# A GNN-and-experts kernel: per-group sums kept as three bf16 parts, and expert tiles taken up in four lots

## The chip, the cores and the metric

The kernel runs on one core of a Trainium2 chip, as one program with one launch. The metric is the device time of that core in microseconds (us).

## The reference

There are N = 6250 rows of D = 512 floats, E = 100000 edges sorted by their target, and 8 experts.

```python
def sage(h, Ws, Wn, b):                      # two layers of this
    agg = segment_sum(h[src], dst, N)        # sum over each row's incoming edges
    deg = segment_sum(1, dst, N)
    return relu(h @ Ws + (agg / max(deg, 1)) @ Wn + b)

x = x + sage(sage(layernorm(x), ...1), ...2)
t = layernorm(x)
top2 = top_k(t @ Wg, 2); gate = softmax(top2 values)
y_e = layernorm(relu(t @ W1[e] + b1[e]) @ W2[e] + b2[e]) * gamma[e] + beta[e]
x = x + sum over the two chosen e of gate_e * y_e
```

All is in float32. The kernel brings in the experts only for the rows that chose them: 12500 row copies, sorted by expert into 105 tiles of 128 rows.

## The kernel before, in words

**Stages.** (0) The layer norm of `x` is written to `xn_d`. (1) The first sums: `sums(xn_d, ...)` with `layer1` as what follows each block. (2) The second sums: `sums(z2, ...)` with `route`, and with work on expert tiles mixed in by `each`. (3) The final loop over the expert tiles that are left, and the gathering of results.

**Sums (L200 to L311).** The 782 tiles of 128 edges are worked in 197 slots, four tiles a slot. Per tile GpSimd issues one indirect DMA (`gather`, L220) that brings 128 rows of 512 floats; VectorE makes a slot's 0/1 matrices `hot` (L230); TensorE adds the four tiles into four strips of 32 rows of the accumulator `pa` (`add`, L248). Three slots make a group, and `close` copies `pa` to SBUF (`st_`, L256): a strip of sums of up to 128 neighbouring rows. A block of 128 rows of the graph needs the three or four groups that `reach` names, 153 pairs of block and group in each sums. `prepare` makes for each pair the 0/1 matrix `sel` (L273, and for the first sums a bf16 copy, L277); `take_out` multiplies it with the strip (L285), so that the block's sums stand in one PSUM tile. The 49 blocks close three to twelve slots, at distances of 3, 3 and 6.

The order on TensorE, VectorE, ScalarE and GpSimd is the program's own (`manual_schedule`). A slot `i` issues the gathers for a later slot (two on in the second sums, where the ring has 12 buffers; three on in the first, with 16), what `each` gives, `build(i + 2)`, `add(i)`, then what is due at place "mid", then `close`, then what is due at "post". `at(i + k, place, what)` puts something k slots on. SP's queue has no order by hand.

**What follows a block.** In the first sums `layer1`: `u0` the own share for blocks below NS = 36, `u1` transposes, `u2` times Wn1, `u3` transposes, `u4` times Wn2 to `z2` through a tile `z` with one buffer (L576), `u5` times Ws2 to `s2` through a tile `s` with one buffer (L583); the last four `u5` come after the loop. Each of these products is four float32 matmuls, which the trace shows as eight instructions. In the second sums `route`: the sum is finished on VectorE (L987, L988), normalized (L182 to L187, L995), turned, and multiplied with Wg; the two experts are chosen (`experts`), ranked, and the row is sent to each expert's list in `xs` by two indirect DMAs (L975). In the first 48 slots `each` also gives the product of the 36 own shares with Ws2 (`share_of`, L907).

**Expert tiles.** `take_up` on VectorE turns the counts so far into a list of tiles that are full already. It runs when the blocks in `TAKE` are through: blocks 16, 27 and 38, which free 24, 46 and 68 tiles in all. From then on `each` starts one tile at every even slot (`Up`): `fetch` from `xs`, `turn_x` 3 slots on, `times` (W1, L818) 5 on, `turn_h` 6 on. Tiles in `soon` (odd numbers, 34) are finished in the sums as well (`Down`): the product with W2 (L852) and the row b2 by a bf16 matmul (L846) 8 slots on, statistics (L858) 9 on, scaling and the rows gamma and beta (L846, in the two PSUM buffers `ph`) with the products y\*g and +b on VectorE (L876, L877) 10 on. The others store their hidden rows in `hd` and get their `Down` in the final loop.

**The final loop** takes the 71 tiles left: 34 whose hidden rows are read back from `hd` (one `Down` each), then 37 that get both `Up` and `Down`. Meanwhile GpSimd makes the last list (`list_rest`, `places`), and from a given tile on the results are gathered (L1075) and added (L1085).

Of the kernel before, what the change touches and what calls it, by code (L numbers as in the profile page):

```python
# [29 lines left out]
F32 = mybir.dt.float32  # L30
# [37 lines left out]
def gnn_moe(ctx, tc, x, src, dst, Ws1, Wn1, gb1, Ws2, Wn2, gb2, Wg, W1, b1, W2, b2, gamma, beta, out):  # L68
# [131 lines left out]
    def sums(z, pool, pap, room, pn, finish, ring, nring, each=None):  # L200

        nslot = (NG - 1) * TS + min(TS, NT_E - (NG - 1) * NQ * TS)
        ahead = nring // NQ - 1
        tiles = [[t for t in range(i // TS * NQ * TS + i % TS, min(NT_E, (i // TS + 1) * NQ * TS), TS)]
                 for i in range(nslot)]
        gathered, hots, few, strips, counts, sels, sels_h, due = {}, {}, {}, {}, {}, {}, {}, {}  # L210
        pa = [None]

        def at(i, place, what):
            due.setdefault((i, place), []).append(what)

        def gather(i):
            if i < nslot:
                for t in tiles[i]:
                    gathered[t] = ring()
                    nc.gpsimd.indirect_dma_start(  # L220
                        out=gathered[t], out_offset=None, in_=z[:, :],
                        in_offset=bass.IndirectOffsetOnAxis(ap=srcT[:, t : t + 1], axis=0))

        def build(i):
            if i >= nslot:
                return
            g, j = divmod(i, TS)
            m = len(tiles[i])
            hots[i] = pool.tile([P, NQ, SW], F32, name="hot", bufs=4)
            nc.vector.tensor_tensor(  # L230
                hots[i][:, :m],
                rel.rearrange("p (c j) -> p j c", j=TS)[:, j, g * NQ : g * NQ + m]
                .rearrange("p (t o) -> p t o", o=1).to_broadcast([P, m, SW]),
                iota_row[:, :SW].rearrange("p (o m) -> p o m", o=1).to_broadcast([P, m, SW]), OP.is_equal)
            if pn is not None and j:

                end = j == TS - 1 or i == nslot - 1
                few[g] = pool.tile([P, NQ, SW], BF16 if end else F32, name=f"few{int(end)}", bufs=1)
                before = hots[i - 1] if j == 1 else few[g, 1]
                nc.vector.tensor_add(few[g][:, :m], before[:, :m], hots[i][:, :m])  # L240
                few[g, j] = few[g]

        def add(i):
            g, j = divmod(i, TS)
            if pa[0] is None:
                pa[0] = pap.tile([P, D], F32, name="pa", bufs=2)
            for q, t in enumerate(tiles[i]):
                nc.tensor.matmul(pa[0][q * SW : (q + 1) * SW], hots[i][:, q], gathered.pop(t), start=(j == 0),  # L248
                                 stop=(j == TS - 1 or t == NT_E - 1), tile_position=(0, q * SW))

        def close(i):

            g = i // TS
            k = len(tiles[i]) * SW
            st = pool.tile([P, D], F32, name="st_", bufs=most)
            nc.scalar.copy(st[:k], pa[0][:k])  # L256
            strips[g] = st, k
            pa[0] = None
            if pn is not None:
                nc.tensor.matmul(pn[:k, 0], few[g].rearrange("p q m -> p (q m)")[:, :k], halves,  # L260
                                 start=True, stop=True)
                counts[g] = pool.tile([P, NDEG], BF16, name="counts", bufs=most + 1)
                nc.vector.tensor_copy(counts[g][:k], pn[:k, 0])
            for b in range(NB):
                if reach[b][1] == g:
                    at(i + 1, "mid", lambda b=b: prepare(b))
                    at(i + 1, "post", lambda b=b: take_out(i + 1, b))

        def prepare(b):
            for g in range(reach[b][0], reach[b][1] + 1):  # L270
                k = strips[g][1]
                sels[b, g] = pool.tile([P, P], F32, name="sel", bufs=most)
                nc.vector.tensor_scalar(sels[b, g][:k], iota_row[:k], float(b * P), node[:k, g : g + 1],  # L273
                                        op0=OP.add, op1=OP.is_equal)
                if pn is not None:
                    sels_h[b, g] = pool.tile([P, P], BF16, name="sel_h", bufs=most)
                    nc.vector.tensor_copy(sels_h[b, g][:k], sels[b, g][:k])  # L277

        def take_out(i, b):
            a, z = reach[b]  # L280
            ps = room()
            for g in range(a, z + 1):
                st, k = strips[g]
                sel = sels.pop((b, g))
                nc.tensor.matmul(ps, sel[:k], st[:k], start=(g == a), stop=(g == z))  # L285
                if pn is not None:
                    nc.tensor.matmul(pn[:, 1], sels_h.pop((b, g))[:k], counts[g][:k], start=(g == a), stop=(g == z))
# [36 lines left out]
    NT = (2 * N + NE * (P - 1)) // P  # L324
    NT0 = (2 * N + P - 1) // P
    SLOTS = NE * R + (NT - NT0) * P
    TAKE = [NB // 3, 27 * NB // 49, 38 * NB // 49]
    upto_n = [(2 * b * P - NE * (P - 1)) // P for b in TAKE]
    n0 = [0] + upto_n

# [1 line left out]
    NTAKE = len(TAKE) + len(LEVEL) + 1  # L332

    NCL = [(2 * b * P + NE * (P - 1)) // P for b in LEVEL]
    soon = [j for j in range(upto_n[-1]) if j % 2]
    xs = dram.tile([SLOTS, D], F32, name="xs")
    hd = dram.tile([upto_n[-1], P, D], F32, name="hd")
    ys = dram.tile([NT * P, D], F32, name="ys")
# [199 lines left out]
    with tc.tile_pool(name="s1", bufs=2, side="right") as pool, \  # L538
# [6 lines left out]
        def layer1(b, pa, pd):  # L545
# [27 lines left out]
            def u4():  # L573
                pz = psp.tile([P, D], F32, name="pm")
                project(pz, own["hT"], wn2, True, True)
                t = pool.tile([P, D], F32, name="z", bufs=1)  # L576
                nc.scalar.copy(t, pz)
                nc.sync.dma_start(z2[r], t[:n])

            def u5():  # L580
                ps = psp.tile([P, D], F32, name="pm")
                project(ps, own["hT"], ws2, True, True)
                t = pool.tile([P, D], F32, name="s", bufs=1)  # L583
                nc.vector.tensor_add(t, ps, bb2)
                nc.sync.dma_start(s2[r], t[:n])

# [211 lines left out]
    class Up:  # L798
# [9 lines left out]
            tc.add_to_no_dep_group("xs", inst.ins)  # L808

        def turn_x(self):  # L810
            self.xT = transposed(self.pool, self.psp, self.xg, AF.Copy,
                                 out=self.pool.tile([P, C, P], F32, name="xgT", bufs=1))

        def times(self):
            _, self.e = read(eof, self.i, [ENG.PE, ENG.DVE], NE - 1)
# [66 lines left out]
    with tc.tile_pool(name="s2", bufs=2, side="right") as pool, \  # L882
# [45 lines left out]
        def route(b, pa):  # L928
# [10 lines left out]
            def logits():  # L939
                pl = psp.tile([NE, P], F32, name="small", bufs=1)  # L940
                for c in range(C):
                    nc.tensor.matmul(pl[:, :n], wg[:, c, :], t["xT"][:, c, :n], start=(c == 0), stop=(c == C - 1))
                t["lT"] = pool.tile([NE, P], F32, name="lT", bufs=1)
                nc.scalar.copy(t["lT"][:, :n], pl[:, :n])

            def experts():
# [41 lines left out]
            nc.vector.scalar_tensor_tensor(acc[:n], a[:n], 0.0, acc[:n], op0=OP.max, op1=OP.add)  # L988
            nc.sync.dma_start(accs[r], acc[:n])
            for e in range(NE):  # L990
                if b == (1 + 3 * e if e < NE // 2 else NB // 4 - 3 + e):
                    load_w2(e)
            mv, rs = norm_stats(pool, acc[:n], n)
            t["xn"] = part(NW + (13, 14, 16)[b % 3])
# [8 lines left out]
        def each(i):  # L1003
# [11 lines left out]
                return []  # L1015
            up_next[0] += 1
            u = Up(j, pool, psp, keep=j not in soon)
            u.fetch()
            todo = [(3, "mid", u.turn_x), (5, "mid", u.times), (6, "mid", u.turn_h)]
            if j in soon:  # L1020
                d = {}

                def begin():
                    d[0] = Down(j, u.hT, u.e, pool, psp, pool.tile([P, D], F32, name="y", bufs=1))
                    d[0].rows = {"gamma": "ph", "beta": "ph"}
                    d[0].times()
# [325 lines left out]
```

## Time and profile before

| | us |
|---|---|
| three runs | 2961.6, 2962.2, 2971.19; median 2962.2 |
| profiled execution, time | 2965.84 |
| profiled execution, span of the profile | 2964.1 |
| TensorE matmul busy | 2710.7 (91%) |
| GpSimd busy | 1846.4 (62%) |
| VectorE busy | 1203.8 (41%) |
| ScalarE busy | 616.8 (21%) |
| first gather of the first sums, first of the second, last of the second | 116.9, 1139.0, 2311.5 |
| first product of the final loop | 2431.6 |

An engine's busy time is the union of its instructions. TensorE's instructions are pipelined and each is shown until its modelled end, so an instruction that is started alone looks longer than one of a dense row. The starts of neighbouring instructions tell what each costs. A name such as `big<-z,srcT` is the written tile and the read ones; `big` is one large SBUF tile that is used in parts of 512 floats (`part`). DMA issues are not counted as an engine's busy time, but GpSimd's indirect ones are shown, since it makes their descriptors.

### The profile page before, as it was taken

The page shows a single profiled execution, that of the slowest core. Times are in us where ns is not written, and L with a number is a line of the kernel's source. Part 1 is how long each engine was busy: PE and PEld are TensorE (multiplying, and loading weights), DVE is VectorE, ACT ScalarE, POOL GpSimd, SP SyncE. Part 2 cuts the span into 40 slices and gives each one's busy share as a digit, 9 for nine tenths or more (in the row PEclk, how much of TensorE's full clock was granted, in tenths as well). Part 3 has the DMA queues.
Part 4 walks back from the last instruction along what each step waited for, and adds up shares of the span by engine and source line. Part 5 has one row for each costly group of instructions (what it writes and reads, how often), then busy time and mean ns, then how long its engine had stood idle before and what let it go on. Part 6 is the DMA issues. An engine that isn't in the chain of part 4 may idle for free. (4 is left out here: it accounts for less than half of the span.)

```text
span 2964.1 us, 33569 instructions
## 1 busy us (share of the span) xinstructions
PE 2710.7 (91%) x9704; PEld 1063.8 (36%) x9704; DVE 1203.8 (41%) x4163; ACT 616.8 (21%) x1127; POOL 1846.4 (62%) x2116
## 2 busy tenths in 40 slices
PE   6899999999999997999878999999899889999994
PEld 3333333333333332333212333333333333344441
DVE  6522222222222221343334445444544436544775
ACT  2211111111111110111112333333233312222221
POOL 5377777777777763777777777677677128200543
PEclk9999999999999998999999999999999989999997
DMA  6778888888877765999888888888788324312986
GB/s 229 246 241 249 250 247 250 275 251 249 245 238 234 238 208 180 324 325 324 270 283 275 283 276 270 263 264 264 242 271 267 123 86 149 115 60 69 303 292 209
DMA packets 269818, 699.12 MB, mean 236 GB/s; under 512 B 43036, under 2 KB 43150, under 8 KB 269596
## 3 DMA queue, kind: packets, MB, share of 16 engines
q0 software_dynamic: 144000, 464.43, 51.0%
q1 hardware_dynamic: 121964, 225.61, 22.0%
q10 hardware_dynamic: 3664, 6.85, 0.7%
q8 instruction: 83, 1.36, 0.2%
q14 instruction: 107, 0.88, 0.1%
HBM read 557.23 MB, written 140.28 MB: 235 GB/s over the span
## 5 line engine op out<-in xcount | busy, mean ns | idle before, releaser
L220 POOL DMA_INDIRECT big<-z,srcT x782 | 752.4, 962 | 340.3 <-issue 145.3
L220 POOL DMA_INDIRECT rows_t<-xn_d,srcT x782 | 743.3, 950 | 286.6 <-issue 112.8
L852 PE MATMUL py<-w,hT 128*128 x840 | 392.6, 611 | 16.8 <-DMA hT<-hd 8.6
L248 PE MATMUL pa<-big,hot 128*32 128x512 f32 x1564 | 321.9, 621 | 60.1 <-DMA big<-z,srcT 45.0
L552 PE MATMUL pm<-wn,tT 128*128 128x512 f32 x752 | 347.7, 605 | 0.6 <-ACT tT L196 0.6
L818 PE MATMUL ph<-big,xgT 128*128 x544 | 268.1, 638 | 38.8 <-DVE y L876 38.4
L248 PE MATMUL pa<-rows_t,hot 128*32 128x512 f32 x1564 | 271.0, 609 | 29.5 <-DMA rows_t<-xn_d,srcT 27.3
L1075 POOL DMA_INDIRECT big<-ys,yrow x98 | 107.7, 1099 | 293.9 <-DMA ys<-y 197.0
L852 PEld LDWEIGHTS py<-w,hT 128*128 128x128 f32 x840 | 152.8, 192 | 217.5 <-issue 172.9
L552 PEld LDWEIGHTS pm<-wn,tT 128*128 128x128 f32 x752 | 135.2, 189 | 213.2 <-issue 173.1
L818 PEld LDWEIGHTS ph<-big,xgT 128*128 128x128 f32 x544 | 103.9, 201 | 199.3 <-issue 135.1
L829 DVE TENSOR_SCALAR hT<-pt,b1T 128x128 f32<-128x128 f32 x272 | 76.7, 344 | 165.1 <-PE pt L826 161.8
L552 PE MATMUL pm<-ws,big 128*128 128x512 f32 x320 | 143.5, 592 | 0.0
L975 POOL DMA_INDIRECT xs<-big,slot x98 | 99.1, 1012 | 71.1 <-DVE slot L971 50.9
L907 PE MATMUL ph<-w 128*128 128x512 f32 x288 | 135.1, 613 | 4.2 <-DMA w<-in_L_gnn_W_self 4.2
L1115 PE MATMUL ph<-big,xgT 128*128 x296 | 136.9, 605 | 0.0
L248 PEld LDWEIGHTS pa<-big,hot 128*32 128x32 f32 x1564 | 49.3, 109 | 224.7 <-DMA big<-z,srcT 146.7
L566 DVE SCALAR_TENSOR_TENSOR h<-pm,rcnt,big 128x512 f32<-128x512 f32 x49 | 36.8, 750 | 220.5 <-PE pn L260 209.7
L557 DVE TENSOR_TENSOR big<-pm,bb 128x512 f32<-128x512 f32 x36 | 24.9, 692 | 246.7 <-PE pm L552 246.7
L987 DVE SCALAR_TENSOR_TENSOR big<-ph,rcnt,big 128x512 f32<-128x512 f32 (+1 forms) x49 | 36.8, 751 | 216.6 <-PE ph L285 216.6
L230 DVE TENSOR_TENSOR hot<-rel,iota_row 128x128 f32<-128x128 bf16 (+1 forms) x394 | 107.8, 283 | 31.6 <-PE pa L248 14.2
L858 DVE BATCH_NORM_STATS2 st<-py 128x6 f32<-128x512 f32 x105 | 73.0, 695 | 107.6 <-PE py L846 107.6
(653 smaller groups left out, 3321.7 us busy)
## 6 DMA issues: line engine op xcount, KB each, us to landing
xg<-xs SPq DMA_DIRECT2D x105, 256.0 KB
ys<-y SPq DMA_DIRECT2D x105, 256.0 KB
rows_t<-xn_d,srcT POOLq DMA_INDIRECT x782
big<-z,srcT POOLq DMA_INDIRECT x782
z<-z SPq DMA_DIRECT2D x48, 256.0 KB
xa<-in_x SPq DMA_DIRECT2D x48, 256.0 KB
big<-s SPq DMA_DIRECT2D x48, 256.0 KB
accs<-xa SPq DMA_DIRECT2D x48, 256.0 KB
```

Of the source, the lines that this page charges most:

```text
L220: nc.gpsimd.indirect_dma_start(out=gathered[t], out_offset=None, in_=z[:, :], in_offset=bass.IndirectOffsetOnAxis(ap=srcT[:, t : t + 1], a ...
L230: nc.vector.tensor_tensor(hots[i][:, :m], rel.rearrange("p (c j) -> p j c", j=TS)[:, j, g * NQ : g * NQ + m] .rearrange("p (t o) -> p t o" ...
L248: nc.tensor.matmul(pa[0][q * SW : (q + 1) * SW], hots[i][:, q], gathered.pop(t), start=(j == 0), stop=(j == TS - 1 or t == NT_E - 1), tile ...
L552: nc.tensor.matmul(ph, tT[:, c], w[:, c], start=(start and c == 0), stop=(stop and c == C - 1))
L818: nc.tensor.matmul(ph, self.xT[:, c], w1[:, bass.ds(self.e * KD + c * D, D)], start=(c == 0), stop=(c == C - 1))
L829: nc.vector.tensor_scalar(hT[:, c], pt[:, c], b1T[:, bass.ds(self.e * HC + c, 1)], 0.0, op0=OP.add, op1=OP.max)
L852: nc.tensor.matmul(self.py, self.hT[:, c], w2[:, bass.ds(self.e * KD + c * D, D)], start=(c == 0), stop=False)
L858: nc.vector.bn_stats(st, self.py)
L907: nc.tensor.matmul(ps, hT[:, c], ws2[:, c], start=(c == 0), stop=(c == C - 1))
L975: inst = nc.gpsimd.indirect_dma_start(out=xs[:, :], out_offset=bass.IndirectOffsetOnAxis(ap=slot[:n, b, k : k + 1], axis=0), in_=t["xn"][: ...
L1075: nc.gpsimd.indirect_dma_start(out=yk[:n], out_offset=None, in_=ys[: ready[0] * P, :], in_offset=bass.IndirectOffsetOnAxis(ap=yrow[:n, b, ...
L1115: nc.tensor.matmul(ph, u.xT[:, c], w1[:, bass.ds(u.e * KD + c * D, D)], start=(c == 0), stop=(c == C - 1))
```

## The change

1. **Take-outs in bf16 thirds.** `close` rounds the strip to bf16 (`st[0]`). One slot on, at "mid", `rest` subtracts that from `pa` in PSUM, rounds what is left (`st[1]`), and subtracts again (`st[2]`). `take_out` does three bf16 matmuls for each pair in place of one float32 matmul. `sel` is made in bf16 at once, and the copy L277 goes. `take_out` moves from "post" one slot on to "mid" two slots on.
2. **z and s rows in free parts of `big`**, instead of tiles with one buffer each; the transposed tile `xgT` takes the place of `xg`; `lT` goes into a part; `hot` has 3 buffers in the second sums instead of 4.
3. **Four lots of tiles:** at blocks 12, 20, 29 and 38, which free 16, 32, 50 and 68 tiles.
4. **Two of three tiles** of these 68 are finished in the second sums: 45 instead of 34.
5. **Order:** `fetch` comes at the end of its slot; `times`, `turn_h` and the product with W2 one slot earlier; scaling and the rows gamma and beta earlier too. The last four loads of W2 come one block earlier.

```diff
@@ build
-            hots[i] = pool.tile([P, NQ, SW], F32, name="hot", bufs=4)
+            hots[i] = pool.tile([P, NQ, SW], F32, name="hot", bufs=3 if pn is None else 4)
@@ close, prepare, take_out
-            st = pool.tile([P, D], F32, name="st_", bufs=most)
-            nc.scalar.copy(st[:k], pa[0][:k])
+            st = [pool.tile([P, D], BF16, name=f"st_{h}", bufs=most) for h in range(3)]
             strips[g] = st, k
+            nc.scalar.copy(st[0][:k], pa[0][:k])
+            at(i + 1, "mid", lambda pa=pa[0]: rest(st, k, pa))
...
-                    at(i + 1, "post", lambda b=b: take_out(i + 1, b))
+                    at(i + 2, "mid", lambda b=b: take_out(i + 2, b))
+
+        def rest(st, k, pa):
+            nc.vector.tensor_sub(pa[:k], pa[:k], st[0][:k])
+            nc.scalar.copy(st[1][:k], pa[:k])
+            nc.vector.tensor_sub(st[2][:k], pa[:k], st[1][:k])
...
-                sels[b, g] = pool.tile([P, P], F32, name="sel", bufs=most)
+                sels[b, g] = pool.tile([P, P], BF16, name="sel", bufs=most)
...
-                if pn is not None:
-                    sels_h[b, g] = pool.tile([P, P], BF16, name="sel_h", bufs=most)
-                    nc.vector.tensor_copy(sels_h[b, g][:k], sels[b, g][:k])
...
-                nc.tensor.matmul(ps, sel[:k], st[:k], start=(g == a), stop=(g == z))
+                for h in range(3):
+                    nc.tensor.matmul(ps, sel[:k], st[h][:k], start=(g == a and h == 0), stop=(g == z and h == 2))
@@ tables
-    TAKE = [NB // 3, 27 * NB // 49, 38 * NB // 49]
+    TAKE = [12 * NB // 49, 20 * NB // 49, 29 * NB // 49, 38 * NB // 49]
-    soon = [j for j in range(upto_n[-1]) if j % 2]
+    soon = [j for j in range(upto_n[-1]) if j % 3]
@@ layer1
-                t = pool.tile([P, D], F32, name="z", bufs=1)
+                t = part(b if b < NB - LATE else b - LATE)
...
-                t = pool.tile([P, D], F32, name="s", bufs=1)
+                t = part(b - 1 if b < NB - LATE else b)
@@ Up.turn_x
-                                 out=self.pool.tile([P, C, P], F32, name="xgT", bufs=1))
+                                 out=self.xg.rearrange("p (c n) -> p c n", c=C))
@@ route
-                t["lT"] = pool.tile([NE, P], F32, name="lT", bufs=1)
+                t["lT"] = part(NW + 15)[:NE, :P]
...
-                if b == (1 + 3 * e if e < NE // 2 else NB // 4 - 3 + e):
+                if b == (1 + 3 * e if e < NE // 2 else NB // 4 - 4 + e):
@@ each
-            u.fetch()
-            todo = [(3, "mid", u.turn_x), (5, "mid", u.times), (6, "mid", u.turn_h)]
+            todo = [(0, "post", u.fetch), (3, "mid", u.turn_x), (4, "mid", u.times), (5, "mid", u.turn_h)]
...
-                todo += [(8, "mid", begin), (9, "mid", lambda: d[0].spread()), (10, "mid", lambda: d[0].scale()),
-                         (10, "post", lambda: (d[0].affine(), d[0].finish()))]
+                todo += [(7, "mid", begin), (8, "mid", lambda: d[0].spread()), (8, "post", lambda: d[0].scale()),
+                         (9, "post", lambda: (d[0].affine(), d[0].finish()))]
```

More of the change, by code (lines that the diff above doesn't have):

```diff
@@ L209, in sums @@
                  for i in range(nslot)]
-        gathered, hots, few, strips, counts, sels, sels_h, due = {}, {}, {}, {}, {}, {}, {}, {}
+        gathered, hots, few, strips, counts, sels, due = {}, {}, {}, {}, {}, {}, {}
         pa = [None]
@@ L284, in take_out @@
                 sel = sels.pop((b, g))
-                nc.tensor.matmul(ps, sel[:k], st[:k], start=(g == a), stop=(g == z))
+                for h in range(3):
+                    nc.tensor.matmul(ps, sel[:k], st[h][:k], start=(g == a and h == 0), stop=(g == z and h == 2))
                 if pn is not None:
-                    nc.tensor.matmul(pn[:, 1], sels_h.pop((b, g))[:k], counts[g][:k], start=(g == a), stop=(g == z))
+                    nc.tensor.matmul(pn[:, 1], sel[:k], counts[g][:k], start=(g == a), stop=(g == z))
             for behind, place, what in finish(b, ps) if pn is None else finish(b, ps, pn[:, 1]):
```

## The prediction

> **What bounds the kernel now.** I read the page first, then the groups by line, the windows, the chain of waits by engine, and single slots in order of time. The page:
>
> ```profile
> PE 2710.7 (91%) x9704; PEld 1063.8 (36%) x9704; DVE 1203.8 (41%) x4163; ACT 616.8 (21%) x1127; POOL 1846.4 (62%) x2116
> PE   6899999999999997999878999999899889999994
> L220 POOL DMA_INDIRECT big<-z,srcT x782 | 752.4, 962 | 340.3 <-issue 145.3
> L220 POOL DMA_INDIRECT rows_t<-xn_d,srcT x782 | 743.3, 950 | 286.6 <-issue 112.8
> ```
>
> TensorE looks like the bound everywhere. In the first sums it is not. There GpSimd's gathers take 743.3 us and have 286.6 us before them, 47.1 of it one wait ahead of the first (chain of waits). So 982.8 us hold 782 gathers: 1.257 us each, 0.95 of work and 0.30 of issue. The first starts at 116.9 and the last at 1098.8: no gap. GpSimd sets the pace, 5.03 us a slot, and TensorE merely fits in.
>
> The second sums have two halves. Windows (PE, PEld, DVE, ACT, POOL, clock, DMA), and three pieces in order of time:
>
> ```profile
> 1450.00:1500.00 50.00, 40.04 (x116) 10.25 (x116) 17.59 (x84) 8.29 (x15) 38.44 (x44) 0.97 0.78 243
> 2050.00:2100.00 50.00, 46.34 (x198) 19.78 (x197) 22.04 (x83) 14.51 (x28) 36.25 (x42) 1.00 0.85 273
> 2430.00:2570.00 140.00, 138.16 (x339) 51.78 (x339) 85.39 (x210) 32.18 (x60) 95.73 (x184) 0.97 0.44 140
> ```
> ```profile
> 1496.03 1.05 PE L248 MATMUL pa<-big,hot 128*32 128x512 f32 x2 [0.39 <-DMA big<-z,srcT]
> 1497.37 1.04 PE L248 MATMUL pa<-big,hot 128*32 128x512 f32 x2 [0.29 <-DMA big<-z,srcT]
> ...
> 2054.50 1.07 PE L248 MATMUL pa<-big,hot 128*32 128x512 f32 x8
> ...
> 2062.06 0.37 PE L846 MATMUL ph<-gamma,its 24*128 24x512 bf16 x1
> 2062.28 0.37 PE L846 MATMUL ph<-beta,its 24*128 24x512 bf16 x1
> ...
> 2065.90 3.70 PE L818 MATMUL ph<-big,xgT 128*128 x8 [2.25 <-DVE y L876]
> ...
> 2077.01 1.13 PE L285 MATMUL ph<-st__13706,sel 128*128 128x512 f32 x2 [1.41 <-DVE sel L273]
> 2077.97 1.02 PE L285 MATMUL ph<-st__13870,sel 128*128 128x512 f32 x2
> 2078.83 1.02 PE L285 MATMUL ph<-st__14044,sel 128*128 128x512 f32 x2
> ```
>
> Around 1496 a slot's add comes in pairs that wait for their gathers: each pair is "busy" for 1.04 us, though at 2054 all four pairs take 1.07. The 80% of the first window are therefore mostly idle: with 0.99 for an add, 0.87 a strip and 1.35 a block's routing, slots 48 to 73 hold about 2.1 us of real TensorE work in 5.5. GpSimd sets the pace there too: 48 gathers of 1.254 and three pairs of row sends (2.6 us each beyond a gather) make 68 us for 12 slots, 5.67 a slot. From slot 74 (about 1565 us) on the expert tiles run and TensorE decides: from slot 84 to 192 12 slots take 75 us. In the final loop it is dense: 4.38 us a tile from `hd`, 8.96 a tile with both halves.
>
> **The change part by part.** *Take-outs.* A strip costs 0.87 us (2077.97 to 2078.83). gamma to beta is 0.22 between starts, also bf16 with 512 columns; three make 0.65. Alone such a matmul is shown for 0.37, so 1.11 is the other end. I take 0.65: the three stand in a dense row with the same weights. That is 0.22 saved on each of 153 pairs in either sums. In the first sums it is worth nothing while GpSimd paces: 0.
>
> The Trainium skill ("TensorE: Matmul & The Clock Gate", Back-to-back issue gap) gives about 131 ns for a sustained stream with 512 columns, against the 0.22 us between gamma and beta here; by it three would take 0.39 and the second sums would save 0.26 more on each pair, 40 us. The starts here decide.
>
> *The split.* Each of the 131 groups gets two subtractions (0.69 each, by L877, which reads PSUM too) and one ScalarE copy (0.59, L256). In the first sums 152 casts (0.256) go. Both engines have room; what counts is order. DVE waits between the two subtractions for ScalarE, where the copy stands behind `u4`'s or `turn`'s. Queued behind on DVE: `sel`, scaling, hT, later `hot`. The take-out gets a slot for it. In the first sums, behind `u2`'s row (0.75): subtraction, copy, subtraction, `sel` are ready 3.2 us after `u2`, TensorE needs them after 1.55 (add, `u3`): 1.6 us late, three times in 12 slots. TensorE's work there is 4.31 us a slot with the new strips (4.48 now), so 51.7 + 4.9 + about 2 of other waits = 58.6, against GpSimd's 60.3. It fits, narrowly.
>
> More DVE work can slow the making of descriptors: a gather takes 950 ns in the first sums and 962 in the second, where DVE is about twice as busy. 12 ns times 782 is 9 us at most; 0 to 9, I take 2 within the margin below.
>
> The Trainium skill ("SBUF — State Buffer", SBUF: two separate sides) says that GpSimd can't write descriptors while DVE runs a two-port mode, which speaks against more DVE work beside gathers. If every one of the 66 x 1.38 us of subtractions in the first sums shut it out, that would be 91 us as an estimate; the 12 ns above say that little of this is seen.
>
> *z and s in parts.* The end of the first sums:
>
> ```profile
> 1146.19 0.69 DVE L584 TENSOR_TENSOR s<-pm,bb 128x512 f32<-128x512 f32 x1 [3.79 <-DMA s<-s]
> 1157.50 2.79 PE L248 MATMUL pa<-big,hot 128*32 128x512 f32 x12 [13.10 <-DVE hot L230]
> 1159.65 0.95 POOL L220 DMA_INDIRECT big<-z,srcT  x1 [5.97 <-PE pa L248]
> ```
>
> The last s store leaves its one buffer late, lands about 1156.6 among the gathers, and every engine's first step in the next stage waits for it. TensorE is done at 1144.4, four gathers land about 1146. With s outside, the 13th gather does not wait: 5.97 - 0.30 = 5.7 us; the rest is under GpSimd's pace. Bounds 0 to 6, I take 6. The tail's extra slot costs 2 us of split and saves 2 of waiting for `sel`: 0. `xgT`, `lT` and the third `hot` buffer wait for steps a slot back: 0, up to 2 us. The last W2 load now lies 2 slots ahead of the first product with W2: up to 10 us once; with the descriptors I put 4 for both.
>
> *Tiles earlier and more of them.* By the lists, the first tile starts at slot 60, not 74, the last at 200, not 208, and the loop ends after slot 209, not 218. Slots 60 to 196 now: 137 adds 136, 106 strips 92, routing 46, 59 `Up` of 4.52 (3.54 + 0.43 + 0.55) 267, 29 `Down` of 4.38 127; sum 668. They take 845 (1486 to 2331): 51 is the light part before slot 74, 126 are waits, 1.02 a slot. After: 136 + 69 + 46 + 64 x 4.52 + 41 x 4.38 = 720. Waits: the slots become even (4.5 to 6.9 us instead of 2.1 to 8.7), and `sel` is ready a slot ahead (1.4 to 1.9 less a take-out). But gamma and beta take both `ph` buffers, and the next `times` waits until DVE has done y\*g. In 12 slots this falls twice behind `experts` (1.7 us, now 2.25) and twice behind a take-out, whose row needs 3.6 us on DVE first (3.0 each): 9.4 for the 6.2 that I count now. Even slots give some back. Bounds 0.7 and 1.5 a slot, I take 1.1: 151, and 6 for the light slots to 70, where GpSimd paces: 877, 32 more than now.
>
> *What is left behind the last gather.* Now 98 us (2331 to the first fetch at 2428.9), 67 of it work. After: 4 `Down`, 4 `times` and small things, 41, with waits by slots (31 x 13/22) 59: 39 less.
>
> *Final loop.* 11 tiles fewer from `hd`, dense, 4.38 each: 48 less. The list for its later tiles is ready 34 us after its start (GpSimd, 2429 to 2463) and is first read 83 us after it (19 x 4.38), so it stays hidden.
>
> **Sum:** -6 + 4 + 32 - 39 - 48 = -57; 2965.8 becomes 2909, and against the median (3.6 below the profiled time) about 2905.
>
> **The rivals.** *GpSimd keeps the pace* (20%): if the even slots lose little, slots 60 to 196 need only 137 x 5.67 = 777, 100 less: 2805, with half of it 2855. For: 12 slots hold 66.5 of work against GpSimd's 68. Against: `ph` waits can't be hidden in one ordered queue.
>
> *The moved tiles cost what they save* (20%): 1.35 a slot, +34: 2939; with strips at 1.11 each, which would mean that bf16 thirds do not shorten the take-out at all, 49 more on 106 strips, 2954.
>
> *Slower: the split comes last at the take-out* (10%). DVE and ScalarE hand over three times; if every take-out waits W us longer than above, the first sums absorb 0.5 a block and pay (W - 0.5) x 49, the second pay W x 34. It decides from W = 1.0 (24 + 34 = 58); at 2 it is 141 - 57 = +84: 3046. For: 28.2 us of waiting for y between 1600 and 2330 show that DVE's order already stalls TensorE. Against: ScalarE is 21% busy.
>
> **How the numbers follow.** The forecast itself has 50%. Its own range is 1.1 +- 0.4 a slot, 2850 to 2960; half of the first rival lies inside, and what is left out below is the rest of it, above the slower one: I give 2845 to 2955. About 0.3%, 9 us, is what a measurement can tell from no change. Faster than 2953: the forecast, the first rival and most of the second, 0.86; within: 0.05; slower: 0.09.
>
> **What would show it.** Right: gathers of the first sums still 1.254 apart; the 13th gather of the second without the 6 us; strips 0.65 apart; the first `Up` near 1490; slot 197 near 2358; the final loop 48 shorter. Wrong: pauses between gathers of the first sums; take-outs that wait for the second subtraction; `ph` waits above 13 us per 12 slots; a final loop that waits for its list.

## The result and the profile after

The changed kernel takes 3125.3 us (median of four runs, 3120.4 to 3128.6) against 2966.2 for the kernel before (2961.6 to 2971.2): 1.0532 times, interval 1.0513 to 1.0551. Predicted were 2905 us, in a range from 2845 to 2955. It is 159 us slower. The profiled execution took 3120.35 us, its span 3118.2.

The page of the changed kernel, with the rows that answer to those shown of before, the granted clock and the two groups of tile products:

```profile
PE 2704.3 (87%) x10010; PEld 1061.7 (34%) x10010; DVE 1342.6 (43%) x4313; ACT 681.4 (22%) x1257; POOL 1853.2 (59%) x2129
PE   6899999999999989998788788778878887999994
...
PEclk8999999999999999999899988988889888999997
...
L220 POOL DMA_INDIRECT big<-z,srcT x782 | 750.6, 960 | 552.3 <-PE pa L248 306.0
L220 POOL DMA_INDIRECT rows_t<-xn_d,srcT x782 | 743.6, 951 | 284.4 <-issue 118.6
L858 PE MATMUL py<-w,hT 128*128 x840 | 429.4, 658 | 74.4 <-ACT y L876 54.1
L824 PE MATMUL ph<-big,xg 128*128 x544 | 299.6, 702 | 87.9 <-DVE y L882 72.9
```

The last two groups before:

```profile
L852 PE MATMUL py<-w,hT 128*128 x840 | 392.6, 611 | 16.8 <-DMA hT<-hd 8.6
L818 PE MATMUL ph<-big,xgT 128*128 x544 | 268.1, 638 | 38.8 <-DVE y L876 38.4
```

TensorE is busy for the same time as before (2704 against 2711 us) in a span that is 154 us longer. What grew is the idle time in slices 19 to 33, the second sums. There the gathers now wait for TensorE (552 us idle ahead of them, 340 before), and the clock row has more eights. The first sums' gathers are what they were.

The stages, by the starts of TensorE's instructions in the two traces:

| stage | before, us | after, us | change | predicted |
|---|---|---|---|---|
| up to the first add of the second sums | 1157.5 | 1145.7 | -11.8 | -6 |
| slots 0 to 60 | 328.5 | 335.5 | +7.0 | part of +4 |
| slot 60 to the last add | 843.5 | 1064.1 | **+220.6** | +32 |
| last add to the first product of the final loop | 102.1 | 86.2 | -15.9 | -39 |
| final loop's products | 491.4 | 444.5 | -47 | -48 |
| rest | 41.1 | 42.2 | +1 | 0 |

One stage holds the whole miss. The windows of just that stage (us, then busy time and count of PE, PEld, DVE, ACT and POOL, the granted clock, DMA share, GB/s), before:

```profile
1486.00:2329.50 843.50, 761.52 (x3072) 306.44 (x3072) 404.00 (x1633) 239.80 (x422) 596.08 (x684) 0.96 0.82 265
```

and after:

```profile
1481.20:2545.30 1064.10, 861.68 (x3387) 345.51 (x3387) 499.32 (x1864) 280.95 (x497) 594.12 (x680) 0.90 0.68 210
```

Idle time of TensorE rose from 82.0 to 202.4 us (+120.4), busy time by 100.2, and the mean clock fell from 0.96 to 0.90. My sum had 52 us more work (720 against 668). So about 120 of the 221 us are pauses, about 50 are the work that I counted, and about 50 are work that took longer than before. The list of TensorE's waits in that stage says which pauses they are (us in total, times, longest). Before:

```profile
PE ph L818 <- DVE y L876: 28.2, 11, 5.0
...
PE ph L285 <- DVE sel L273: 11.5, 8, 1.6
```

After:

```profile
PE ph L824 <- DVE y L882: 65.4, 34, 2.2
PE py L858 <- ACT y L876: 45.4, 19, 3.8
...
PE ph L290 <- DVE sel L280: 9.0, 8, 3.4
```

The take-outs do not wait longer than before (9.0 us against 11.5): it is not the split at the take-out. The wait for `y` in front of W1 has grown, from 11 times to 34, and a second one has come that the kernel before did not have: the product with W2 waits for ScalarE to have read the one `py` buffer. The two make 82.6 of the 120 us. Waits for ScalarE's copy of a transposed tile add 27.5 (29.4 us in 24 waits, before 1.9); the rest is spread over small ones. TensorE in order of time (start, us, engine, line, operation, tiles, and in brackets the wait ahead of it):

```profile
2228.11 0.37 PE L852 MATMUL ph<-beta,its 24*128 24x512 bf16 x1
2228.42 1.06 PE L248 MATMUL pa<-big,hot 128*32 128x512 f32 x8
2231.16 5.34 PE L824 MATMUL ph<-big,xg 128*128 x8 [1.68 <-DVE y L882]
...
2245.97 6.47 PE L824 MATMUL ph<-big,xg 128*128 x8 [2.16 <-DVE y L882]
2252.36 1.06 PE L248 MATMUL pa<-big,hot 128*32 128x512 f32 x8
2253.36 3.70 PE L858 MATMUL py<-w,hT 128*128 x8
```

The rows gamma and beta take both `ph` buffers, one add follows, and then the next product with W1 needs one of them back. It waits for about 2 us, and then takes 5.34 or 6.47 us in place of the 3.70 that the same eight instructions take at 2253. The windows of the last two products show why (the clock is the third figure from the end):

```profile
2245.97:2252.36 6.39, 6.39 (x8) 2.50 (x8) 1.23 (x4) 0.00 (x0) 3.53 (x4) 0.56 0.92 312
2253.36:2257.00 3.64, 3.64 (x13) 1.45 (x9) 0.00 (x0) 0.24 (x1) 2.71 (x3) 1.00 0.64 160
```

The first ran at a granted clock of 0.56, the second at 1.00. The pause costs its own 2.16 us and 2.8 more behind it. In this stage 24 of 63 products with W1 and 14 of 41 with W2 took over 4.5 us (before: 5 of 59 and 0 of 28), and what they took beyond 3.70 sums to 77.5 us (before 10.6). That is 67 us more, above the 50 by which busy time outgrew the counted work, because the adds, fewer of which now stand alone in pairs, are shown shorter (156 us, before 188). TensorE was at half clock for 211.6 us of it, before for 61.4.

The wait for `py`, with VectorE's queue beside it:

```profile
2267.32 1.06 PE L248 MATMUL pa<-big,hot 128*32 128x512 f32 x8
2267.43 0.75 DVE L993 SCALAR_TENSOR_TENSOR big<-ph,rcnt,big 128x512 f32<-128x512 f32 x1 [4.16 <-PE ph L290]
2268.21 0.69 DVE L994 SCALAR_TENSOR_TENSOR xa<-big,xa 128x512 f32<-128x512 f32 x1
...
2268.94 0.69 DVE L182 BATCH_NORM_STATS2 st<-xa 128x6 f32<-128x512 f32 x1
...
2270.41 0.55 DVE L1001 TENSOR_SCALAR big<-xa,mv,rs 128x512 f32<-128x512 f32 x1
2270.87 0.16 DVE L871 RECIPROCAL rs<-rs 128x1 f32<-128x1 f32 x1
2271.07 0.21 DVE L873 TENSOR_SCALAR nm<-mv,rs 128x1 f32<-128x1 f32 x1
...
2271.31 0.78 ACT L876 ACTIVATE y<-py,nm,rs 128x512 f32<-128x512 f32 x1 [1.14 <-DVE nm L873]
...
2272.14 1.22 PE L858 MATMUL py<-w,hT 128*128 x1 [3.76 <-ACT y L876]
```

The scaling of the tile before (L871 to L876) is two tiny steps and one pass, but the new order puts it at "post", and there the finish of the block (L993 to L1001) stands ahead of it in VectorE's queue. It needs 3.4 us from 2267.43 on, and TensorE, which wants the `py` buffer at 2268.4, stands until 2272.1. With two of three tiles finished on the way, two of them follow each other two slots apart; with every second one they never did.

In all runs of the experiments every kernel took longer than in this comparison, the kernel before too (3361 to 3390 us against 2966), for a cause that is open; so a variant is set only against the kernel before on the same chip, and a stage only against stages of those runs. The traces of those runs show 15 to 19% fewer updates of TensorE's semaphore than instructions that make one, and many updates 3 us and more behind their instruction, so there the name of what a wait was for, and its total, are less certain than here.

### The profile page after: what moved, and what is told of

It reads as the page before. It is cut to its first block, busy times and chain, and to the rows that moved or that the text cites. A ratio compares the mean times of both kernels' runs of the same rounds, so it can differ in the third digit from the quotient of the medians.

```text
span 3118.2 us, 34382 instructions
## 1 busy us (share of the span) xinstructions
PE 2704.3 (87%) x10010; PEld 1061.7 (34%) x10010; DVE 1342.6 (43%) x4313; ACT 681.4 (22%) x1257; POOL 1853.2 (59%) x2129
## 3 DMA queue, kind: packets, MB, share of 16 engines
q1 hardware_dynamic: 118796, 219.84, 20.5%
## 5 line engine op out<-in xcount | busy, mean ns | idle before, releaser
L858 PE MATMUL py<-w,hT 128*128 x840 | 429.4, 658 | 74.4 <-ACT y L876 54.1
L824 PE MATMUL ph<-big,xg 128*128 x544 | 299.6, 702 | 87.9 <-DVE y L882 72.9
L248 PE MATMUL pa<-big,hot 128*32 128x512 f32 x1564 | 297.4, 621 | 36.7 <-DMA big<-z,srcT 35.7
L858 PEld LDWEIGHTS py<-w,hT 128*128 128x128 f32 x840 | 166.5, 209 | 303.6 <-issue 202.6
L824 PEld LDWEIGHTS ph<-big,xg 128*128 128x128 f32 x544 | 115.8, 224 | 275.2 <-issue 205.4
L274 DVE TENSOR_TENSOR st<-pa,st 128x512 bf16<-128x512 f32 x132 | 91.2, 691 | 192.2 <-ACT st L273 192.2
L273 ACT CAST st<-pa 128x512 bf16<-128x512 f32 x132 | 77.2, 585 | 420.1 <-DVE pa L272 419.9
L981 POOL DMA_INDIRECT xs<-big,slot x98 | 100.1, 1021 | 102.1 <-DVE slot L977 82.1
L290 PE MATMUL ps<-st,sel 128*128 128x512 bf16 (+1 forms) x459 | 111.3, 381 | 40.1 <-DVE sel L280 40.1
L1120 PE MATMUL ph<-big,xg 128*128 x296 | 136.9, 605 | 0.0
L290 PEld LDWEIGHTS <-sel 128*128 128x128 bf16 (+1 forms) x918 | 75.6, 98 | 161.9 <-DVE sel L280 67.0
L290 PE MATMUL ph<-st,sel 128*128 128x512 bf16 (+1 forms) x459 | 110.7, 388 | 9.1 <-DVE sel L280 9.0
```

Source lines behind the costliest of these rows:

```text
L273: nc.scalar.copy(st[1][:k], pa[:k])
L274: nc.vector.tensor_sub(st[2][:k], pa[:k], st[1][:k])
L290: nc.tensor.matmul(ps, sel[:k], st[h][:k], start=(g == a and h == 0), stop=(g == z and h == 2))
L824: nc.tensor.matmul(ph, self.xT[:, c], w1[:, bass.ds(self.e * KD + c * D, D)], start=(c == 0), stop=(c == C - 1))
L858: nc.tensor.matmul(self.py, self.hT[:, c], w2[:, bass.ds(self.e * KD + c * D, D)], start=(c == 0), stop=False)
L981: inst = nc.gpsimd.indirect_dma_start(out=xs[:, :], out_offset=bass.IndirectOffsetOnAxis(ap=slot[:n, b, k : k + 1], axis=0), in_=t["xn"][: ...
```

## Experiments

Theory O: the new order of the tiles' steps makes TensorE wait for `y` and for the one `py` buffer, and the pauses lower its clock. Rival S: the hand-overs of the split cost it. Rivals N and lots: the mere number of tiles, or the lots that come earlier.

**One part undone at a time.** Each is a single run of the changed kernel with one part put back; the kernel before took 3384.5 us beside the first four and 3380.0 beside the fifth, also in single runs. Nineteen runs of the kernel before on one chip (the next group) spread over 37 us, so differences of some 30 us between two single runs are at the edge of what can be told.

Float32 take-outs, with their place ("post", one slot on) and `sel_h` as before:

```diff
-                for h in range(3):
-                    nc.tensor.matmul(ps, sel[:k], st[h][:k], start=(g == a and h == 0), stop=(g == z and h == 2))
+                nc.tensor.matmul(ps, sel[:k], st[:k], start=(g == a), stop=(g == z))
...
```

> The changed kernel with the take-outs of before put back (one float32 strip, sel in float32 with its bf16 copy, take-out one slot on at post); all else as changed. Theory O (the new order of the tiles' steps makes TensorE wait for VectorE and ScalarE at the one py and the two ph buffers, and the pauses let the granted clock fall): slots 60 to 196 keep at least 7.5 us each, total 3070 to 3160, since about 25 us of strips come back. Rival S (the split's hand-overs between VectorE and ScalarE are what is late): the slots fall to about 6.3 us and the total to 2880 to 2950.

Measured: 3413.5 us, 29 above the kernel before.

Every second tile:

```diff
-    soon = [j for j in range(upto_n[-1]) if j % 3]
+    soon = [j for j in range(upto_n[-1]) if j % 2]
```

> The changed kernel with every second tile of the first 68 finished in the second sums, as before (34 instead of 45). Theory O: the products with W2 are then four slots apart and not two, so the waits for the one py buffer (54 us in the changed kernel) go, those for ph fall by a quarter; the slots fall to about 6.9 us, minus 150 in the second sums, plus 48 in the final loop: 2990 to 3050. Rival S: the hand-overs stay, 3080 to 3150. Rival N (it is the mere number of tiles): 11 x 4.4 us less in the sums and as much more in the final loop, 3100 to 3130.

Measured: 3415.6 us, 31 above.

The order of before, with two of three tiles:

```diff
-            todo = [(0, "post", u.fetch), (3, "mid", u.turn_x), (4, "mid", u.times), (5, "mid", u.turn_h)]
+            u.fetch()
+            todo = [(3, "mid", u.turn_x), (5, "mid", u.times), (6, "mid", u.turn_h)]
...
-                todo += [(7, "mid", begin), (8, "mid", lambda: d[0].spread()), (8, "post", lambda: d[0].scale()),
-                         (9, "post", lambda: (d[0].affine(), d[0].finish()))]
+                todo += [(8, "mid", begin), (9, "mid", lambda: d[0].spread()), (10, "mid", lambda: d[0].scale()),
+                         (10, "post", lambda: (d[0].affine(), d[0].finish()))]
```

> The changed kernel with the order of before for the tiles' steps (fetch at the start of its slot, times 5, turn_h 6, product with W2 8, statistics 9, scaling and affine 10 slots on), xg still turned in place; thirds, four lots, and two of three tiles stay. Theory O: the scaling is then ahead of the finish of a block on VectorE, the waits for py and most of those for ph go, the slots fall to 6.4 to 6.9 us and the total to 2900 to 2970. Rivals S and N: at least 3080.

> The same kernel as e3_old_order (the changed kernel with the order of before for the tiles' steps), where before itself took 3384 us, so that no row compares with the profiles of before and after. Theory O: 2900 to 2970 where before takes 2966. Rivals S and N: at least 3080.

Measured: 3420.2 us, 36 above, and on the other chip 3419.3 us, 39 above.

Thirds and free parts alone: order, three lots, every second tile and the W2 loads of before, all put back (`xgT` stays in `xg`'s place; the order as in the edit above):

```diff
-    TAKE = [12 * NB // 49, 20 * NB // 49, 29 * NB // 49, 38 * NB // 49]
+    TAKE = [NB // 3, 27 * NB // 49, 38 * NB // 49]
-    soon = [j for j in range(upto_n[-1]) if j % 3]
+    soon = [j for j in range(upto_n[-1]) if j % 2]
...
```

> Thirds and the free parts alone: order of the tiles' steps, three lots and every second tile as before. Theory O: no slower than before, 2930 to 2970 (the strips save 0.22 us each, the stage's start 6 to 12 us). Rival S: the second sums are slower by over 1 us a slot, 3050 or more.

Measured: 3383.0 us, 1.5 below.

The expectations were written against 2966 us; against the kernel before of each run they read so. The float32 take-outs (29 above) fit neither theory (O 104 to 194 above, S 16 to 86 below). Every second tile (31 above) fits O (24 to 84 above), not S or N (114 and more). The order of before (36 and 39 above) is a miss of O, which had at most 4. Thirds and parts alone (1.5 below) fit O and not S (84 or more above).

What follows: thirds and parts are harmless in the order of before, so rival S falls in its plain form. But "the old order" is no cure by itself: with two of three tiles its scaling, 10 slots on at "mid", meets the next tile's product with W2, which is 8 slots on and starts two slots later, and TensorE waits for `py` there too (59.2 us in 15 waits in the whole trace, 82.3 in 17 on the other chip). As far as single runs tell, no single part of the change carries the loss; order and number act together. What is missing here is the changed kernel itself beside them, and an edit of one step of the order in place of six.

**One step of the order.** First the changed kernel on the chip of the next two:

> The changed kernel itself, beside the kernel before on the same chip, so that its stages can be set against those of the variants under the same conditions. Whatever the theory: if the conditions are those of the first comparison, 3125 us against 2966. If the kernel before takes about 3380 us again, as it did beside the first variants, theory O (the order of the tiles' steps makes TensorE wait for y and for the one py buffer) expects this kernel well above it, by 60 us or more; if nearly all of the 159 us goes away where the first sums too are held up by TensorE, the loss lay in what the two have in common there, and less than 40 us is left.

Measured: 3446.0 us (3435.1 to 3448.4) against 3360.6; 1.0266 times, 1.0232 to 1.0301: 85 us above, not 159. Why the loss is smaller here is open; the kernel before now has pauses of its own in that stage (214.5 us idle by its trace below, 82.0 in the first comparison), with which the new ones can coincide.

Scaling at "mid" of the same slot, ahead of the finish of the block:

```diff
-                ... (8, "mid", lambda: d[0].spread()), (8, "post", lambda: d[0].scale()),
+                ... (8, "mid", lambda: d[0].spread()), (8, "mid", lambda: d[0].scale()),
```

> The changed kernel with one step moved: scaling (L871 to L876) at place mid of its slot, 8 slots on, instead of at post behind the finish of the block. Theory O, with the wait for the one py buffer as a large part (22 waits, 54.1 us, each followed by a product at the lower clock): 50 to 90 us faster than the changed kernel. If the wait for y in front of W1 (37 waits, 72.9 us) is the larger part, 10 to 40 us faster, since that wait is untouched. Rival S (the hand-overs of the split) expects no difference.

Measured: 3364.9 us, 1.0030 times the kernel before (1.0002 to 1.0058): 81 us less than the changed kernel. The wait for `py` is gone from the stage; that for `y` stays:

```profile
PE ph L824 <- DVE y L882: 58.3, 24, 6.2
```

One place in a list is worth 81 of the 85 us, as theory O had it for a `py` wait that is a large part (50 to 90).

The order of before and every second tile, with thirds, parts and four lots:

```diff
-    soon = [j for j in range(upto_n[-1]) if j % 3]
+    soon = [j for j in range(upto_n[-1]) if j % 2]
...
```

with the order as in the third edit above.

> The changed kernel with the order of the tiles' steps of before and every second tile finished on the way as before; thirds, free parts and four lots stay. Theory O: the second sums lose the waits for py and about half of the waits for y; all in all within 20 us of the kernel before, 130 to 170 us faster than the changed one. Rival S: 100 us or more above the kernel before, since the split is still in. Rival lots (the tiles that come earlier take up the slots in which the gathers were ahead): 30 to 60 us above the kernel before.

Measured: 3349.1 us, 0.9972 (0.9945 to 0.9998), 97 us less than the changed kernel: well below what I expected of it (130 to 170 less), since the loss itself is smaller here, but at the kernel before as the theory said. Rival S (100 above) and the rival of the lots (30 to 60 above) fall.

**The second step, and both.** The rows gamma and beta one slot earlier, at "post" of the slot of the scaling, so that the next product with W1 comes a slot and a half behind them; once with the scaling at "mid" and once alone:

```diff
-                         (9, "post", lambda: (d[0].affine(), d[0].finish()))]
+                         (8, "post", lambda: (d[0].affine(), d[0].finish()))]
```

> The changed kernel with scaling at place mid of its slot (8 slots on) and the rows gamma and beta at post of the same slot in place of the next one, so that the next product with W1 comes a slot and a half after them instead of right after them. Theory O: the wait of TensorE for y in front of W1 (65 us with the scaling alone moved) falls below 25 us, and the kernel is 25 to 60 us faster than with the scaling alone moved, so 20 to 50 us faster than the kernel before. If the price was the number of tiles, not their order: no change against the scaling alone, the kernel before plus or minus 10 us.

> The changed kernel with only the rows gamma and beta a slot earlier; scaling stays at post, behind the finish of the block. Theory O: the wait for py stays (40 us and more, each followed by a product at the lower clock), the wait for y becomes shorter; 10 to 40 us faster than the changed kernel, still 40 to 75 us above the kernel before.

Measured, against 3390.4 us of before: both 3344.8, 0.9876 (0.9841 to 0.9911), 46 us below; rows alone 3400.0, 1.0017 (0.9990 to 1.0044), 10 above, which is not told apart from no difference. Both together did what was expected. The rows alone did more: I had left 40 to 75 us above the kernel before to the wait for `py`, and it is 10. With the rows alone the wait for `y` in front of W1 is gone from the stage, and that for `py` stays:

```profile
PE py L858 <- ACT y L876: 22.8, 11, 2.7
```

Both early, and the float32 take-outs of before:

> As the kernel with both steps early, but with the take-outs of before: one float32 product a pair, no split on VectorE and ScalarE. By my sum of durations the thirds save 0.22 us on each of 106 pairs, so this one is 23 us slower than with both steps early. Rival S (the split's hand-overs cost more than the thirds save): 20 us or more faster.

Measured: 3367.8 us, 0.9925 (0.9897 to 0.9954): 23.0 us slower than with the thirds. My sum of durations said 0.22 x 106 = 23. That the figures agree so closely is in part luck: of the 27.6 us between the two traces 13.2 lie in the stage for which the 106 pairs were counted, 13.6 before it. In the changed order the float32 version had been the better one (29 above the kernel before in its single run, the thirds 72 to 85, on other chips). By its trace TensorE waited for `y` 8 times in the stage (33.8 us), where the changed kernel on another chip did so 28 times (69.7): there the split seems to have stood in the queue behind which TensorE's next steps waited, though the take-outs' place changed with it. So the thirds are a gain in the repaired order; that it is nothing but their durations is not shown.

The kernel before, for its stages under these conditions:

> The kernel before, for its trace under the conditions of these runs, so that its stages stand beside those of the variants. No theory differs on it: as long as the runs of the kernel before beside it, within 0.5%. If it is near 3360 us, its first sums too last 1180 us rather than 985, since those of all variants did.

Measured: 3374.8 us, span 3373.0; its first sums end at 1300 us as those of the variants do.

**All on one chip, and the number of tiles.**

> The changed kernel once more, to stand beside the next two on one chip. Theory O with the two moved steps: 60 us or more above the kernel before here too. If the conditions are those of the first comparison, 159 us above it.

> The changed kernel with scaling and the rows gamma and beta early, beside the changed kernel on the same chip. Theory O: 100 us or more below the changed kernel and 30 to 60 us below the kernel before. If the gain of 1.2% over the kernel before was the chip's, it is within 10 us of the kernel before.

> As the kernel with both steps early, but with every second tile finished on the way in place of two of three: 11 tiles more in the final loop, dense there, 4.38 us each, +48. If the tiles fit between the gathers once the order is right, this one is 10 to 48 us slower than with two of three; if the number of tiles was a price of its own (each taking more than 4.38 us of the second sums), it is equal or faster.

Measured, against 3363.4 us of before: changed 3435.6, 1.0216 (1.0175 to 1.0258); both early 3323.0, 0.9867 (0.9807 to 0.9928), 113 us below the changed kernel and 40 below the one before; both early with every second tile 3345.8, 0.9954 (0.9926 to 0.9982), 23 more than with two of three. By the traces the 11 tiles take 42 us in the final loop and 29 in the sums: they pay once the order lets them in. In the changed order it was the other way round (31 above the kernel before with every second, in a single run; 72 to 85 with two of three).

The two steps make four kernels. Their stage from slot 60 to the last add, by the traces (two where there are two); a product is long above 4.5 us:

| kernel | stage, us | wait for `y` before W1 | wait for `py` | long W1, of 63 | long W2, of 41 |
|---|---|---|---|---|---|
| changed | 1137.0, 1127.8 | 69.7 (second trace) | 34.1 | 30, 29 | 15, 14 |
| scaling early | 1065.1 | 58.3 | none | 27 | 2 |
| rows early | 1092.3 | none | 22.8 | 9 | 13 |
| both early | 1037.4, 1034.5 | none | none | 10, 13 | 4, 2 |
| kernel before | 995.0 | 38.8 | none | 18 of 59 | 0 of 28 |

Each step takes away its own wait and most of the long products behind it, and leaves most of the other's. TensorE's idle time in the stage, from the same traces, is 258 us in the changed kernel, 227 with the scaling early, 254 with the rows early, 202 and 210 with both, and 214.5 in the kernel before; its time at half clock, in the same order, is 313 and 300, 229, 242, 216 and 223, and 222. So the rows alone gave back clock rather than idle time: other waits, one of 20.5 us for `sel` among them, stand in that trace in place of the wait for `y`. In total time they overlap in part: the scaling alone is worth 81 us, the rows alone 62 to 75 (72 to 85 above the kernel before becomes 10, on another chip), both 113. TensorE's waits in the stage, changed kernel (third time):

```profile
PE ph L824 <- DVE y L882: 69.7, 28, 5.8
PE py L858 <- ACT y L876: 34.1, 10, 3.8
```

and both early, where neither is left and the first line is a wait for the transposed tile:

```profile
PE ph L824 <- ACT xg L196: 40.8, 9, 6.9
```

TensorE with both early, in order of time:

```profile
2247.26 0.38 PE L852 MATMUL ph<-gamma,its 24*128 24x512 bf16 x1
2247.62 0.37 PE L852 MATMUL ph<-beta,its 24*128 24x512 bf16 x1
...
2248.06 1.06 PE L248 MATMUL pa<-big,hot 128*32 128x512 f32 x8
2249.05 3.70 PE L858 MATMUL py<-w,hT 128*128 x8
...
2257.04 1.06 PE L248 MATMUL pa<-big,hot 128*32 128x512 f32 x8
2258.04 3.70 PE L824 MATMUL ph<-big,xg 128*128 x8
```

Between the rows and the next product with W1 there are now ten microseconds of other work, the product with W2 among them, and both products take 3.70.

## Why the prediction was wrong, point by point

- **First sums paced by GpSimd, thirds worth nothing there: right.** The gathers run from 116.8 to 1098.2 us, 1.257 apart (predicted 1.254), without a gap. More work on VectorE did not slow them: one takes 951 ns, before 950.
- **z and s in parts, -6: right.** The 13th gather of the second sums no longer waits 5.97 us; it is the second of these rows:

```profile
1153.93 0.94 POOL L220 DMA_INDIRECT big<-z,srcT  x1 [0.30 <-DMA big<-z,srcT]
1155.18 0.95 POOL L220 DMA_INDIRECT big<-z,srcT  x1 [0.30 <-issue]
```

  The first add of the second sums comes 11.8 us earlier and slots 0 to 60 take 7.0 longer, so slot 60 starts 4.8 us earlier than before, where I had 2.
- **Three thirds at 0.65 us: right.** Twelve such matmuls take 2.76 us and nine 2.12, so three cost 0.64; and thirds against float32 are worth 23.0 us with both steps early.
- **Final loop, -48: right** (-47).
- **Slots 60 to the end of the second sums, +32: wrong; this is the step that failed.** The term of the sum was 1.1 us of waits a slot, with bounds 0.7 and 1.5. The stage took 1064.1 us for 720 of counted work: 344 over, 2.5 a slot, where the sum had 157. Two things were missing from the term. First, I looked for waits on `ph` alone. `py` has one buffer, the diff moved the scaling behind the finish of a block and put products with W2 two slots apart; the code before the result shows all three, and I named nobody who waits behind the scaling. It cost 45.4 us of pauses. Second, I priced a wait at its own length. The long products behind the pauses came to 67 us more than before. The trace of before already had them: its five long products with W1 stand behind pauses of 2.3 to 5.0 us. Four others stand behind pauses of 2.25 to 2.33 and take 3.70, and the one that I quoted is of these; I took it for the rule. The length of the waits for `y` was not what I had too small: 9.4 us per 12 slots make 107 in the stage, and they came to 65.4. The rest of the 187 us above the sum, some 75, is not taken apart; the waits for a transposed tile are in it.
- **My alarm was set on the wrong quantity.** "`ph` waits above 13 us per 12 slots" would have stayed silent: the waits for `y`, 65.4 us in 137 slots, are 5.7 per 12, less than the 9.4 that I had allowed, and all waits on `ph` (98.9 us) are 8.7 per 12. What cost is not in that sum: 23 of the 34 waits for `y` were followed by a product with W1 of over 4.5 us, and the waits for `py` are not on `ph`.
- **Behind the last gather, -39: half right.** It became 15.9 shorter. With both steps early the stage goes from 102.1 (kernel before, same conditions) to 67.0 us, 35 less; each step alone gives 74.0 (scaling) and 79.1 us (rows). So the rest of my gain went with the same two places in the order.
- **The rivals.** "GpSimd keeps the pace" is out: the gathers wait 306 us for TensorE. "The moved tiles cost what they save" has the right place, and a price several times its 34 us. "The split comes last at the take-out" has the right sign and the wrong mechanism: the take-outs wait no longer than before. That the split made other steps wait in the changed order is likely by the float32 run, and not shown.
- **What the sum was good for.** For the kernel with both steps early its large terms hold (span 3373.0 to 3327.1, on two chips): -6.7 up to the second sums, -4.6 for slots 0 to 60, +39.5 for the stage that I had at +32, -35.1 behind it, -38.1 in the final loop, -0.9 for the rest; in sum -45.9 where I forecast -57. In that stage busy time grew by 51.6 us (counted: 52) and idle time fell by 12. The other trace of that kernel, on the chip of the kernel before, gives -35.7 in all: next to nothing up to slot 60, then +42.4, -35.3, about -43 and about +1. Each is one trace under the longer conditions, so the agreement of single terms may be chance.
- **Left open.** How far the two steps restore the first comparison's 159 us was not measured under its conditions, where the kernel before took 2966 us; beside the kernel before at 3363 they restore all of the 72 and 40 more. For the 159 us themselves the cause is read from the waits and the clock of one trace.

The Trainium skill ("TensorE: Matmul & The Clock Gate", the closing table on why this matters) warns against gaps of TensorE above about 3 us between bursts, and names one idle window of 3.4 us as what drops the clock (Part 1). It is the rule that spoke against this change, and I did not weigh it. Taken by its figures it would still have passed all 34 waits for `y`, the longest of 2.2 us, though not the eight for `py` of 3.8: the measurement is stricter, as the last section shows.

## What to carry to other kernels

When steps of one queue are reordered, list for each single-buffered tile who frees it and what stands ahead of that step on its engine; a two-instruction step that gives a buffer back belongs ahead of the long ones. Price a pause of TensorE by what the clock does to the work behind it, and look at pauses one by one rather than at their sum. A gain that is real in its own sum of durations (here the thirds, and the tiles moved forward) can be had back by moving the step that it collides with, and that takes fewer lines than undoing the change.

## What the runs showed of the hardware

In the two traces of the first comparison, between slot 60 and the last add, a pause of TensorE of 0.3 to 1.5 us was followed by a half-clock stretch 2 times of 89, one of 1.5 to 2 us 6 times of 18, and one of 2 us or more 45 times of 56 (a stretch counted if it began in the pause or up to 1 us behind it; the pauses are from the modelled end of one instruction to the start of the next). The stretches last 3.41 us or a whole multiple of it.

Why a pause of 2.1 to 2.3 us costs one time and not another shows when these traces are laid on a grid. All 30 and 62 half-clock stretches of the two start on a fixed grid of 3.413 us steps, to within 5 ns. In the same stage, where TensorE stood idle for 60% or more of a step (2.05 us of 3.413, in one pause or several), the next step was at half clock 47 times of 47; where for under 20%, once of 92; in between, 32 times of 104. So in these traces a pause of 2.05 us or more that fell within one step of the grid was followed by half clock every time, and one that straddled two steps could cost nothing: the pause of 2.25 us at 2063.65, which cost nothing, put at most 40% into one step.
